# Two attention layers on one NeuronCore: head values on every other partition, row maxima turned by VectorE, local first pass 6 instead of 3 units ahead

## The chip, the core and the metric

The kernel runs on one core of one Trainium2 chip. The metric is device microseconds of one execution. Before the change the median of 3 runs is 2535.94 us (2533.43 to 2537.54). Engine names are those of the profile: PE is TensorE (PEld its weight loads), DVE is VectorE, ACT is ScalarE, POOL is GpSimd, SP is the engine that issues most DMAs; SPq and ACTq are the DMA queues of SP and ACT.

## The reference

Two layers run one after the other on `x` of shape (2, 2048, 256), that is batch B = 2, T = 2048 tokens, D = 256 features. Each layer normalises, computes an attention branch `s` and a gating branch `g`, and adds their product:

```python
xn = _layernorm(x, axis=-1)
s = _L0_attn_ref(xn, ...)            # 16 heads of 16, softmax over all 2048 keys
g = _silu(_L0_ffn_ref(xn, ...))
x = x + s * g
xn = _layernorm(x, axis=-1)
s = _L1_attn_ref(xn, ...)            # 16 heads of 16, keys at most 64 tokens away
g = _silu(_L1_ffn_ref(xn, ...))
x = x + s * g
```

Both attentions are softmax(q k^T * scale) v over heads of 16 values, followed by an output projection. Layer 0 attends to everything ("global" below), layer 1 only to a band ("local"). The two gating branches are not touched by the change. All values are float32.

## The kernel before

**Heads in strips of 32 partitions.** Four heads (a group g of NG = 4) stand together in one q tile and one k tile, each head on HP = 32 partitions: 16 rows of values (HD = 16), then padding rows. In k the padding rows are 1; in q they are 0, except row 16 of each strip (`HD:P:HP`), in which the kernel writes minus the row maximum of the scores. A product k^T q over the 32 rows then gives the score minus the maximum at once. The padded rows come from DRAM: `qd` has 32 rows per head, whose last 16 are filled early in the kernel (L309) with ones for k and zeros for q, and `fetch` (L581) loads all 128 partitions.

**Two passes over the scores.** An item is (batch b, group g, block n of 512 queries): 32 items in each layer. In the first pass PE computes the scores `sq` and DVE takes their maxima into `mx`; in the second PE computes them again as `sk` with the maximum subtracted, ACT takes exponentials into `e` (in the local layer into `xn` and `elast`), and in the local layer POOL cuts the band with four `affine_select` (L688) per unit. PE multiplies with the values (`acc`, L747), to which a column of ones is added so that a row of the result is the softmax denominator.

**Units and leads.** An item has U units: 16 in the global layer (128 keys each in the second pass), 2 in the local layer (256 queries each). The main loop (L945) runs `s` over units; it emits the second pass of unit `s` together with the first pass of unit `s + U + LEAD`. Work that hangs on a unit is put in the dictionary `after` by `at(s, f, ...)` (L856) and emitted behind that unit. Each engine executes what it is given in order. Instructions wrapped in `pin` stay behind everything emitted before them on their engine; the others are ordered by the framework's scheduler.

**How the maximum gets into q.** Global: `turn_max` (L700) negates the 16 columns of `mx` on DVE (L704) and writes them by a DMA in 4-byte pieces to DRAM (`md`, L705); `fetch_max` (L707) brings them back as rows of 512 (L709) three units later. Local: `place_max` (L714), 3 units before the second pass: PE transposes `mx` (L720), ACT negates it into `row` (L723), and ACT's own queue issues the DMA to q (L726).

**After the second pass** the steps of an item follow at fixed hops: `away` writes all 128 rows of `av` to DRAM (`ad`); `compact` loads the 4 denominators' rows as [128 x 16] and the values into `xn`; `invert` takes the reciprocals on DVE (L786); `write` and `spread` send them through DRAM and broadcast them to 64 partitions (`recb`); `divide` multiplies (L802, on POOL, in the local layer on DVE for every other item). `project` (L830) does the output projection once per block when the last group is done. The last items take `last_there` and `last_back` instead.

**Loads of q and k.** There are two q and two k tiles, for group bg and bg + 1. Global: `fetch(bg + 2)` when bg is done. Local: its first half when bg is half done (L880), its second half when bg is done (L882).

**The order of DVE at the start of an attention.** The pools `kq` (q, k) and `vp` (v) are laid on memory of the stage before; POOL fills v with 1 (L515), then DVE copies the values of batch 0 from PSUM (L535) while PE computes them in a ring of 6 banks (L541).

## Time and profile before

| | us |
|---|---|
| median of 3 runs | 2535.94 |
| the profiled execution, its own time | 2538.34 |
| its span (first to last instruction) | 2536.6 |
| layer norms and gating branch of layer 0 | about 0 to 471 |
| global attention | about 471 to 2115 |
| gating branch of layer 1 | about 2115 to 2225 |
| local attention | about 2225 to 2537 |

The profiled execution took 1.7 us more than its span and 2.4 us more than the median of the runs. A row of the profile gives the source line, the engine, the operation, the names and shapes of output and input (partitions x elements), how many there were, and the busy time in all with the mean of one in ns. Small rows that the change touches:

| what | line | count | mean ns |
|---|---|---|---|
| PE transpose of `mx`, local | L720 | 32 | 277 |
| ACT negation into `row`, local | L723 | 32 | 261 |
| ACT issue of `q<-row` | L726 | 32 | 530 to 1128 (median 545) |
| DVE reduction with mask `seen`, local | L674 | 512 | 410 |
| DVE `divide`, local | L802 | 14 | median 900 |
| DVE copy of values | L535 | 33 | 424 |
| POOL fill of v | L515 | 4 | 4045 |

PE is busy 99% of the span. A busy PE is not PE at its peak: the ends of matmuls are modelled. TensorE's granted clock was 0.999 over the span.

### The profile page before, as it was taken

How to read it: one execution, taken by the hardware profiler on the slowest of the kernel's cores; microseconds unless marked ns; L12 is line 12 of the kernel's file. 1: busy time of each engine (PE TensorE's matmuls, PEld its weight loads, DVE VectorE, ACT ScalarE, POOL GpSimd, SP SyncE). 2: the span in 40 equal slices, each digit the busy share in tenths (PEclk: the TensorE clock that was granted, in tenths of full speed). 3: DMA queues.
4: the chain of work that ended last, by engine and by line, in shares of the span. 5: the costliest groups of instructions: out<-in, count | busy, mean ns of one | idle time of the engine just before them, and what ended most of it. 6: DMA issues, size and time to landing. Idle time of an engine off the chain costs nothing.

```text
span 2536.6 us, 47898 instructions
## 1 busy us (share of the span) xinstructions
PE 2513.1 (99%) x18896; PEld 1060.6 (42%) x18896; DVE 1686.2 (66%) x2747; ACT 1620.8 (64%) x3187; POOL 876.6 (35%) x827
## 2 busy tenths in 40 slices
PE   8999999999999999999999999999999999999999
PEld 6444444444333333333333333333333334457766
DVE  4143333157888888888777788788888765238986
ACT  5400000126888888888888888888888886227755
POOL 0000000102444444444444444444444420016887
PEclk9999999999999999999999999999999999999999
DMA  6131111230001001001001001001000002133552
GB/s 243 50 84 51 52 51 39 82 118 14 14 14 43 16 12 44 16 12 44 16 12 43 10 18 44 12 17 43 15 14 10 14 14 63 49 133 108 163 167 81
DMA packets 146353, 129.83 MB, mean 51 GB/s; under 512 B 93456, under 2 KB 97936, under 8 KB 143568
## 3 DMA queue, kind: packets, MB, share of 16 engines
q1 hardware_dynamic: 144256, 125.46, 16.5%
q8 instruction: 148, 2.42, 0.4%
q10 hardware_dynamic: 1872, 1.31, 0.2%
q14 instruction: 77, 0.63, 0.1%
HBM read 80.50 MB, written 45.97 MB: 50 GB/s over the span
## 4 chain that ended last, share of the span: by engine, by line
PE 79%; DMA 1%; ACT 0%; POOL 0%; DVE 0%; issue 0%; ACTq 0%; SPq 0%; POOLq 0%; DVEq 0%
PE sk L667 25%; PE acc L747 22%; PE sq L667 19%; PE pp L477 5%; PE pr L835 2%; PE pp L532 2%; PE po L1027 1%; PE pt L1023 1%; PE po L1035 1%; PE xb L113 0%; PE xb L138 0%; DMA k<-qd 0%; PE of L827 0%; DMA q<-qd 0%; POOL xn L688 0%
## 5 line engine op out<-in xcount | busy, mean ns | idle before, releaser
L679 DVE TENSOR_REDUCE part<-sq 128x2 f32<-128x1024 f32 x1024 | 1207.3, 1221 | 294.3 <-PE sq L667 284.7
L683 ACT ACTIVATE e<-sk 128x512 f32<-128x512 f32 x2048 | 1058.3, 603 | 217.2 <-PE sq L667 197.7
L667 PE MATMUL sk<-q,k 32*128 32x512 f32 (+2 forms) x5632 | 1135.8, 533 | 1.2 <-ACT xn L683 1.0
L667 PE MATMUL sq<-k,q 32*128 32x512 f32 (+2 forms) x5120 | 1129.1, 569 | 0.5 <-DVE part L679 0.5
L761 POOL TENSOR_TENSOR av<-av,more 128x512 f32<-128x512 f32 x459 | 581.4, 1267 | 936.3 <-ACT more L760 931.1
L667 PEld LDWEIGHTS sk<-q,k 32*128 32x128 f32 x5632 | 522.0, 184 | 604.1 <-ACT e L683 512.5
L747 PE MATMUL acc<-e,v 128*32 128x512 f32 x4096 | 546.7, 605 | 0.0
L667 PEld LDWEIGHTS sq<-k,q 32*128 32x128 f32 x5120 | 402.3, 183 | 22.3 <-DVE part L679 13.2
L760 ACT COPY more<-acc 128x512 f32<-128x512 f32 x459 | 268.7, 585 | 1.2 <-PE acc L747 1.0
L747 PEld LDWEIGHTS acc<-e,v 128*32 128x32 f32 x4096 | 81.8, 108 | 388.2 <-ACT e L683 367.8
L461 ACT ACTIVATE gt<-po 128x512 f32<-128x512 f32 x16 | 8.8, 594 | 321.1 <-PE po L457 321.1
L674 DVE CUSTOM_DVE_ANT_0 seen<-sq,mask 128x256 f32<-128x256 f32 (+1 forms) x512 | 176.2, 410 | 53.6 <-PE sq L667 49.2
L467 POOL TENSOR_TENSOR x<-x,up 128x512 f32<-128x512 f32 x16 | 23.1, 1461 | 450.1 <-DVE up L464 277.5
L448 DVE TENSOR_TENSOR xs<-we,px 128x512 f32<-128x512 f32 x64 | 43.9, 686 | 136.2 <-PE px L440 130.3
L688 POOL TENSOR_SCALAR_AFFINE_SELECT xn<-xn 128x512 f32<-128x512 f32 x172 | 106.2, 652 | 77.4 <-ACT xn L683 75.7
L440 PE MATMUL px<-xn,FV 128*128 128x512 f32 x256 | 121.2, 595 | 0.0
L444 PE MATMUL py<-cum,FW 128*128 128x512 f32 x256 | 120.5, 593 | 0.6 <-DVE cum L412 0.6
L424 PE MATMUL po<-pr,UO 128*128 128x512 f32 x256 | 119.0, 592 | 0.0
L683 ACT ACTIVATE xn<-sk 128x512 f32<-128x512 f32 x172 | 89.8, 602 | 41.1 <-PE sk L667 17.9
L450 DVE TENSOR_TENSOR pr<-xs,py 128x512 f32<-128x512 f32 x64 | 44.0, 687 | 64.8 <-PE py L444 64.6
L424 PEld LDWEIGHTS po<-pr,UO 128*128 128x128 f32 x256 | 48.6, 190 | 61.2 <-issue 61.0
L444 PEld LDWEIGHTS py<-cum,FW 128*128 128x128 f32 x256 | 48.4, 190 | 61.5 <-issue 59.8
(195 smaller groups left out, 1604.0 us busy)
## 6 DMA issues: line engine op xcount, KB each, us to landing
we<-wd SPq DMA_DIRECT2D x128, 128.0 KB
ad<-av SPq DMA_DIRECT2D x59, 256.0 KB
qd<-sb SPq DMA_DIRECT2D x48, 256.0 KB
k<-qd SPq DMA_DIRECT2D x10, 1024.0 KB
q<-qd SPq DMA_DIRECT2D x10, 1024.0 KB
xn<-ad SPq DMA_DIRECT2D x59, 128.0 KB
recb<-rd SPq DMA_DIRECT2D x59, 128.0 KB
q<-qd SPq DMA_DIRECT2D x12, 512.0 KB
```

The source lines that it names most:

```text
L424: nc.tensor.matmul(po[oc], UO[:, ch, bass.ts(oc, P)], pr, start=(ch == 0), stop=False)
L440: nc.tensor.matmul(px, FV[:, c, bass.ts(ch, P)], xn[b][:, c, cols], start=(c == 0), stop=(c == NC - 1))
L444: nc.tensor.matmul(py, FW[:, c, bass.ts(ch, P)], cum[:, c, :], start=(c == 0), stop=(c == NC - 1))
L477: nc.tensor.matmul(ps, w[:, c, bass.ts(hf, P)], xn[b][:, c, bass.ts(n, TB)], start=(c == 0), stop=(c == NC - 1))
L667: nc.tensor.matmul(o, lhs, rhs, start=True, stop=True)
L674: nc.vector.tensor_tensor_reduce(seen[:, lo:hi], sq[:, d, t * 2 * P + lo : t * 2 * P + hi], mask[:, lo:hi], 1.0, LOWEST, ALU.add, ALU.max, ...
L679: nc.vector.tensor_reduce(pt[:, pair[0] : pair[1] + 1, t, kb], sq, AX.X, ALU.max)
L683: nc.scalar.activation(e, t, AF.Exp, scale=scale)
L688: nc.gpsimd.affine_select(out=e[:, :, c, :], in_=e[:, :, c, :], compare_op=ALU.is_ge, fill=0.0, base=0, pattern=[[0, 4], [sign, P]], chann ...
L747: nc.tensor.matmul(acc[hp[j], o : o + hi - lo], vs[b][:, kt, vcols(g, j)], es[j][:, lo:hi], start=(r == 0), stop=(r == len(parts) - 1), sk ...
L760: nc.scalar.copy(more, acc)
L761: nc.gpsimd.tensor_tensor(avs[i], avs[i], more, ALU.add)
```

## The change

- The 16 values of a head stand on the even partitions of its strip (0, 2, ... 30) instead of the first 16. The odd rows 1 to 29 are padding, row 31 (`HP - 1`) holds minus the maximum. `qd` in DRAM has only the 16 value rows; the early writes of ones and zeros to it are gone. Instead DVE fills both k tiles with 1 and both q tiles with 0 at the start of each attention, and `fetch` writes every other partition (64 instead of 128 rows).
- Since `fetch` no longer clears the row of the maximum, the first pass multiplies over 31 rows (`hq`), without row 31.
- The values in v stand on every other column; the denominator comes out on row 15 of a strip (`DEN`).
- In both layers the maxima go by `turn_max` and `fetch_max`; `place_max` is gone. `turn_max` negates into every other column of a [128 x 32] tile, DVE transposes that tile in blocks of 32 by 32, and the DMA to `md` has pieces of 128 bytes.
- `LEAD` of the local layer goes from 3 to 6, the value that the global layer had already.
- `away` sends only the 4 rows of denominators to DRAM; `compact` takes the values from `av` directly. The reciprocals are taken on [32 x 64] instead of [128 x 16]. `spread` broadcasts with the 4 heads outermost. Values stand in the order head, value instead of value, head, so the reordering of the weights on the host goes.

```diff
-        [2, B, H, HP, T], F32, name="qd"
+        [2, B, H, HD, T], F32, name="qd"
...
-        zeros = fw.tile([P, TB], F32, name="zeros")
-        nc.vector.memset(zeros, 0.0)
-        for b in range(B):
-            for i, t in ((0, ones), (1, zeros)):
-                for half in range(NC):
-                    nc.sync.dma_start(
-                        out=qd[i, b, bass.ts(half, H // NC), HD:, :], in_=t[:, None, :].to_broadcast([P, NB, TB])
-                    )
...
-        LEAD = 3 if local else 6
+        LEAD = 6
+        DE = 64
...
-            ad = [dr.tile([NG, HP, TB], F32, name=f"ad{i}", tag=f"ad{i}") for i in range(3)]
+            ad = [dr.tile([NG, TB], F32, name=f"ad{i}", tag=f"ad{i}") for i in range(3)]
...
-            md = [dr.tile([NG * TT, P], F32, name=f"md{i}", tag=f"md{i}") for i in range(2)]
+            md = [dr.tile([NG * TT, NG, HP], F32, name=f"md{i}", tag=f"md{i}") for i in range(2)]
+
+            for k, q in zip(ks, qs):
+                nc.vector.memset(k, 1.0)
+                nc.vector.memset(q, 0.0)
...
+                s = vs[b][p0:p1, c, :]
                 copy(
-                    vs[b][p0:p1, c, : H * HV].rearrange("p (h w) -> p h w", w=HV)[:, :, :HD],
+                    bass.AP(s.tensor, s.offset, [s.ap[0], [HV, H], [2, HD]]),
...
+            hq = [slice(j * HP, (j + 1) * HP - 1) for j in range(NG)]
...
-                    nc.sync.dma_start(out=t[:, to], in_=qd[i, b, bass.ts(g, NG), :, s].rearrange("h w t -> (h w) t"))
+                    nc.sync.dma_start(out=t[::2, to], in_=qd[i, b, bass.ts(g, NG), :, s].rearrange("h w t -> (h w) t"))
...
-                                        q1[hp[j], bass.ts(qt, P)], k1[hp[j], qt * P + lo : qt * P + hi],
+                                        q1[hq[j], bass.ts(qt, P)], k1[hq[j], qt * P + lo : qt * P + hi],
...
+            nmx = [mp.tile([P, NG * TT, 2], F32, name=f"nmx{i}", tag=f"nmx{i}", bufs=1) for i in range(2)]
+            for m in nmx:
+                nc.vector.memset(m, 0.0)
+
             def turn_max(i):
 
                 mx, _ = part.pop(i)
-                nmx = mp.tile([P, NG * TT], F32, name="nmx", tag="nmx")
-                pin(nc.vector.tensor_scalar(nmx, mx.rearrange("p j t -> p (j t)"), -1.0, None, ALU.mult))
-                pin(nc.sync.dma_start(out=md[i % 2].rearrange("j p -> p j"), in_=nmx))
+                m = nmx[i % 2]
+                pin(nc.vector.tensor_scalar(m[:, :, 0], mx.rearrange("p j t -> p (j t)"), -1.0, None, ALU.mult))
+                turned = mp.tile([P, HP], F32, name="tmx", tag="tmx")
+                pin(nc.vector.transpose(turned, m.rearrange("p i e -> p (i e)")))
+                pin(nc.sync.dma_start(out=md[i % 2].rearrange("i s r -> s i r"), in_=turned[::2]))
 
             def fetch_max(i):
 
                 pin(nc.sync.dma_start(
-                    out=tiles(i)[0][HD:P:HP, bass.ts(items[i][2], TB)],
-                    in_=md[i % 2].rearrange("(j t) p -> j (t p)", t=TT),
-                ))
-
-            def place_max(i):
...
+                    out=tiles(i)[0][HP - 1 : P : HP, bass.ts(items[i][2], TB)],
+                    in_=md[i % 2].rearrange("(j t) s r -> j (t s r)", t=TT),
                 ))
...
-                pin(nc.sync.dma_start(out=ad[i % 3].rearrange("j w f -> (j w) f"), in_=avs.pop(i)))
+                pin(nc.sync.dma_start(out=ad[i % 3], in_=avs[i][DEN::HP]))
...
-                divs[i] = op.tile([P, NG * TB // P], F32, name="dn", tag="dn", bufs=3)
-                pin(nc.sync.dma_start(out=divs[i], in_=flat(ad[i % 3][:, HD, :])))
-                pin(nc.sync.dma_start(out=together(*items[i]), in_=ad[i % 3][:, :HD, :].rearrange("j d f -> d j f")))
+                divs[i] = op.tile([NG * TB // DE, DE], F32, name="dn", tag="dn", bufs=3 if local else 1)
+                pin(nc.sync.dma_start(out=divs[i], in_=flat(ad[i % 3])))
+                pin(nc.sync.dma_start(out=together(*items[i]), in_=avs.pop(i)[::2]))
...
-                pin(nc.sync.dma_start(out=divs[i], in_=rd[i % 3][None, :, :].to_broadcast([HD, NG, TB])))
+                pin(nc.sync.dma_start(out=divs[i], in_=rd[i % 3][:, None, :].to_broadcast([NG, HD, TB])))
...
-                if local:
-                    at(i * U - LEAD, place_max, i)
-                else:
-                    at(i * U - LEAD, turn_max, i)
-                    at(i * U - LEAD + 3, fetch_max, i)
+                at(i * U - LEAD, turn_max, i)
+                at(i * U - LEAD + 3, fetch_max, i)
```

More of the change, by code (lines that the diff above doesn't have):

```diff
@@ L25 @@
 HV = HD + 1
+DEN = HD - 1
 TB = 512
@@ L481, in keys_queries @@
         nc.scalar.activation(sb, ps, AF.Identity, bias=bias[:, hf : hf + 1])
-        nc.sync.dma_start(out=qd[i, b, bass.ts(hf, H // NC), :HD, bass.ts(n, TB)], in_=sb)
+        nc.sync.dma_start(out=qd[i, b, bass.ts(hf, H // NC), :, bass.ts(n, TB)], in_=sb)
     def attention(A, scale, local, final, start=None, projected=False):
@@ L663, in scores @@
                                 pieces.append((
-                                    when, sq[:, d], q1[hp[j], bass.ds(n1 * TB + t * P, P)], k1[hp[j], bass.ts(kb, TB)]
+                                    when, sq[:, d], q1[hq[j], bass.ds(n1 * TB + t * P, P)], k1[hq[j], bass.ts(kb, TB)]
                                 ))
@@ L698, in attention @@
             pin = tc.keep_in_program_order
+            nmx = [mp.tile([P, NG * TT, 2], F32, name=f"nmx{i}", tag=f"nmx{i}", bufs=1) for i in range(2)]
+            for m in nmx:
+                nc.vector.memset(m, 0.0)
             def turn_max(i):
                 mx, _ = part.pop(i)
-                nmx = mp.tile([P, NG * TT], F32, name="nmx", tag="nmx")
-                pin(nc.vector.tensor_scalar(nmx, mx.rearrange("p j t -> p (j t)"), -1.0, None, ALU.mult))
-                pin(nc.sync.dma_start(out=md[i % 2].rearrange("j p -> p j"), in_=nmx))
+                m = nmx[i % 2]
[3 more added lines that the diff above has]
+                pin(nc.sync.dma_start(out=md[i % 2].rearrange("i s r -> s i r"), in_=turned[::2]))
             def fetch_max(i):
                 pin(nc.sync.dma_start(
-                    out=tiles(i)[0][HD:P:HP, bass.ts(items[i][2], TB)],
-                    in_=md[i % 2].rearrange("(j t) p -> j (t p)", t=TT),
-                ))
-            def place_max(i):
-                b, g, n = items[i]
-                q = tiles(i)[0]
-                mx, _ = part.pop(i)
-                ps = pm.tile([NG * TT, P], F32, name="pmx", tag="m")
-                nc.tensor.transpose(ps, mx.rearrange("p j t -> p (j t)"), ident)
-                row = mp.tile([NG * TT, P], F32, name="row", tag="row", bufs=2 if local else 1)
-                if local:
-                    pin(nc.scalar.activation(row, ps, AF.Copy, scale=-1.0))
-                else:
-                    nc.vector.tensor_scalar(row, ps, -1.0, None, ALU.mult)
-                pin((nc.scalar if local else nc.sync).dma_start(
-                    out=q[HD:P:HP, bass.ts(n, TB)].rearrange("j (t c) -> j t c", c=P), in_=row
+                    out=tiles(i)[0][HP - 1 : P : HP, bass.ts(items[i][2], TB)],
+                    in_=md[i % 2].rearrange("(j t) s r -> j (t s r)", t=TT),
                 ))
@@ L771, in away @@
             def away(i):
-                pin(nc.sync.dma_start(out=ad[i % 3].rearrange("j w f -> (j w) f"), in_=avs.pop(i)))
+                pin(nc.sync.dma_start(out=ad[i % 3], in_=avs[i][DEN::HP]))
             def flat(d):
-                return d.rearrange("j (r e) -> r j e", r=P // NG)
+                return d.rearrange("j (r e) -> (j r) e", e=DE)
             def compact(i):
-                divs[i] = op.tile([P, NG * TB // P], F32, name="dn", tag="dn", bufs=3)
-                pin(nc.sync.dma_start(out=divs[i], in_=flat(ad[i % 3][:, HD, :])))
-                pin(nc.sync.dma_start(out=together(*items[i]), in_=ad[i % 3][:, :HD, :].rearrange("j d f -> d j f")))
+                divs[i] = op.tile([NG * TB // DE, DE], F32, name="dn", tag="dn", bufs=3 if local else 1)
+                pin(nc.sync.dma_start(out=divs[i], in_=flat(ad[i % 3])))
+                pin(nc.sync.dma_start(out=together(*items[i]), in_=avs.pop(i)[::2]))
             def invert(i):
@@ L810, in last_there @@
                     nc.tensor.transpose(ps[:, t].rearrange("p j w -> p (j w)"), av[:, bass.ts(t, P)], ident)
-                rec = op.tile([P, TT, NG], F32, name="dn", tag="dn", bufs=3)
-                o = divs[i] = op.tile([P, TT, HD, NG], F32, name="over", tag="recb", bufs=2)
-                nc.vector.reciprocal(rec, ps[:, :, :, HD])
+                rec = op.tile([P, TT, NG], F32, name="rec", tag="rec", bufs=2)
+                o = divs[i] = op.tile([P, TT, NG, HD], F32, name="over", tag="recb", bufs=2)
+                nc.vector.reciprocal(rec, ps[:, :, :, DEN])
                 nc.vector.tensor_tensor(
-                    o.rearrange("p t d j -> p t j d"), ps[:, :, :, :HD],
-                    rec[:, :, :, None].to_broadcast([P, TT, NG, HD]), ALU.mult,
+                    o, ps[:, :, :, ::2], rec[:, :, :, None].to_broadcast([P, TT, NG, HD]), ALU.mult
                 )
@@ L822, in last_back @@
                 lo = g % 2 * NG * HD
-                o = divs.pop(i).rearrange("p t d j -> p t (d j)")
+                o = divs.pop(i).rearrange("p t j d -> p t (j d)")
                 ps = pm.tile([P, TB], F32, name="of", tag="m")[lo : lo + NG * HD, :]
@@ L859, in attention @@
             for i, (b, g, n) in enumerate(items):
-                if local:
-                    at(i * U - LEAD, place_max, i)
-                else:
-                    at(i * U - LEAD, turn_max, i)
-                    at(i * U - LEAD + 3, fetch_max, i)
+                at(i * U - LEAD, turn_max, i)
+                at(i * U - LEAD + 3, fetch_max, i)
                 end = (i + 1) * U
@@ L1122, in _attn_arrays @@
 def _attn_arrays(l, wq, wk, wv, bq, bk, bv, wo_t, bo):
-    apart = lambda m: m.reshape(NG, NG, HD, -1).transpose(0, 2, 1, 3).reshape(m.shape)
     cols = lambda v: np.asarray(v).reshape(NC, P).T
@@ L1129, in _attn_arrays @@
         f"wv{l}": wv,
-        f"wo{l}": apart(np.asarray(wo_t).T),
+        f"wo{l}": np.asarray(wo_t).T,
         f"bq{l}": cols(bq),
         f"bk{l}": cols(bk),
-        f"bv{l}": cols(apart(np.asarray(bv))),
+        f"bv{l}": cols(bv),
         f"bo{l}": cols(bo),
```

## The prediction

> **What bounds the kernel now.** I read the page first: engines' shares and the chain that ended last.

> ```profile
> span 2536.6 us, 47898 instructions
> PE 2513.1 (99%) x18896; PEld 1060.6 (42%) x18896; DVE 1686.2 (66%) x2747; ACT 1620.8 (64%) x3187; POOL 876.6 (35%) x827
> ...
> PE 79%; DMA 1%; ACT 0%; POOL 0%; DVE 0%; issue 0%; ACTq 0%; SPq 0%; POOLq 0%; DVEq 0%
> ```

> PE sets the end; DMA, which the change cuts most, has 1% of the chain. Bytes saved are worth nothing by themselves. But 66% for DVE is a mean over stages, so I took busy times by stretches, one in the middle of the global attention, one in the local (columns: stretch, length, then busy us and count of PE, PEld, DVE, ACT, POOL, then clock and DMA):

> ```profile
> 1000.00:1500.00 500.00, 500.00 (x4013) 169.80 (x4008) 400.95 (x371) 421.92 (x829) 221.40 (x175) 1.00 0.08 21
> ...
> 2331.00:2409.00 78.00, 77.43 (x1540) 61.60 (x1544) 71.93 (x399) 57.61 (x132) 66.88 (x102) 1.00 0.52 160
> ```

> Global: DVE 80%, POOL 44%: room. Local: PE 99%, **DVE 92% and POOL 86%**. The starts of `acc` in the timeline give the local item: 2318.17, 2324.57, 2330.96, 2337.47, so 6.47 us (two units) on average, of which DVE works 71.93 / 78 x 6.47 = 5.97. Its slack is 0.5 us per item. That is the number on which the local stage hangs.

> **Global stage: nothing, 0 (-2 to +2).** The first pass with 31 rows must still run four heads side by side. The timeline has products over 16 rows (two accumulators on two strips) beside ones over 128:

> ```profile
> 249.79 1.88 PE L440 MATMUL px<-xn,FV 128*128 128x512 f32 x4
> ...
> 256.75 1.13 PE L457 MATMUL po<-wT,bO 16*128 16x512 f32 x4
> ```

> Four instructions of 16 rows take 1.13 us against 1.88, so a partly filled strip overlaps with its neighbour; 31 rows should too. DVE gains one transpose per item and a longer reciprocal (below), 0.5 us per 46.8 us. In this stage DVE idles 0.57 us in each unit of 2.92 before the next `sq`; the reciprocal of now lowers that idle to 0.41 in its unit, the longer one leaves about 0.1. It fits. Shorter DMAs change nothing: the wait of SP for `md<-nmx` (10 us each, by the waits of SP) is three units ahead and PE has no idle there. The early writes of ones and zeros (8 MB, 33 to 67 us) lie under a PE that is busy 19.90 and 20.00 of 20 us there.

> **Start of the local attention: +3 (0 to +4).** Four fills of 2048 or 2176 columns now stand on DVE ahead of the copies of v. Rows:

> ```profile
> L302 DVE MEMSET ones<- 128x512 f32 x1 | 0.5, 485 | 0.1
> ...
> L557 DVE MEMSET mask<- 128x256 f32 x1 | 0.3, 272 | 0.0
> ```

> (485 - 272) / 256 = 0.83 ns per column and 59 ns fixed: 1.76 for q, 1.87 for k, 7.3 us in all. [...] The memory comes free at 2224.7 (POOL's fill of v waits for `po` until then), DVE finishes its last two updates at 2226.05, so the copies of v start at 2233.3 instead of 2228.95. PE has 6 banks at 0.86 us each, filled at 2230.5; it then waits some 3 us. With one or two fills in DVE's idle time before 2224.4 less is left; at best 0. In the global attention the same fills cost nothing: DVE idles 29.41 us before its first copy of v.

> **The maxima of the local layer.** Gone, per item: on PE a transpose, from its start to the next `sk` 0.20 us (2487.56 to 2487.76); on ACT 0.26 for `row` and 0.55 for the issue of the DMA. ACT has room (57.61 of 78), so this pays only where ACT is blocked. It is, because ACT's queue must wait for the load of q:

> ```profile
> 2463.97 4.83 DMA q<-qd
> 2468.87 0.54 ACTq L726
> ```

> (The chain over this stretch.) Exponentials stand behind that issue, and PE's longest wait, 1.2 us, is there: -1.3 in all. On SP, three units ahead, the fetch blocks nobody's exponentials. Behind the new DMA of `turn_max` on SP stand `write`, `spread` and loads; SP issues some 5 DMAs of 0.55 us per item now, 6 to 7 after, in 6.47 us.

> Added on DVE, per item, each a guess only as far as its row:
> - Reciprocal on 64 columns instead of 16. Rows: 174 ns for 4 columns, 253 for 16, 354 for 32; 6.3 ns per column gives 556 for 64, so **+0.31**.
> - Transpose of [128 x 32]: no row. Below: a fill of 64 columns, 112 ns. [...] Nearest row: a DVE copy of 32 columns, 190. I take 0.2.
> - Negation, 165 ns. But:

> ```profile
> L704 DVE TENSOR_SCALAR nmx<-mx x32: 165/166/1252, 580.2 to 2052.2; 128x16 f32<-128x16 f32 x32
> ...
> 2052.11 1.28 POOL L761 TENSOR_TENSOR av<-av,more 128x512 f32<-128x512 f32 x1 [1.66 <-ACT more L760]
> 2052.17 1.25 DVE L704 TENSOR_SCALAR nmx<-mx 128x16 f32<-128x16 f32 x1
> ```

> All but one took 166 ns; the one that met a POOL instruction took as long as that. [...] This speaks against moving it from ACT to DVE here. I take 0.42; up to 1.5 if it must wait for a whole run of four selects (2.4 us).

> Sum 0.93, less some 0.1 because small DVE instructions overlap (0.17 to the next start where 0.25 is shown): 0.83. DVE then needs 5.97 + 0.83 = **6.80 us per item where the item takes 6.47**. DVE becomes the bound: +0.33. This holds in the items where both passes run and no projection fills PE: 32, less 4 in the run-up, 4 of batch 0's last group and the first: 23 x 0.33 = **+7.6** (bounds: 0.55 added, +1; 1.6 added, +25). In the rest (9 items) PE keeps its 0.20: -1.8.

> **Lead 6 instead of 3: +1.4 (-1 to +3).** Three more first passes before the first exponential, 3 x 1.1 us beside projections that fill PE: +3.3. Three fewer units with both passes: -3 x 3.23. Three more at the end with the second pass alone, where ACT (4 x 0.53 + 0.4) and POOL (2.4 + 0.3) need 2.6: +7.8. What gets tighter: the second half of a k tile, loaded when the group two before ends, is needed at unit 3 instead of 6. Issue 2318.2, need about 2326; k took 5.3 us for 512 KB in the chain, now half the bytes. It fits by 3 to 4 us.

> **Values out of `av`, 4 rows of denominators:** DMAs off the path. [...]

> **Sum** against the execution's own 2538.3: +3.0 + 1.4 + 7.6 - 1.8 - 1.3 = +8.9, 2547.2. That execution lies 2.4 above the median of the runs, so I predict **2544.8**.

> **Rivals.**
> 1. DVE's additions fit into its slack (0.55 or less), and PE's lost transpose counts everywhere: 24 x -0.1 to -0.2, -1.8, -1.3, lead and fills 0 to +2. For it: DVE idles 0.2 to 0.7 us per unit in items without `divide`; against: items with it have none left. 2528 to 2535, say **2532**.
> 2. Slower by one mechanism: the negation waits for POOL's whole run. A `divide` on DVE did so at 2503.59, 5.07 us; against: the median of 14 is 0.90. From 1.0 us of added wait per item it decides: 23 more, **2568**.
> 3. Loads of q and k late with the greater lead, because SP stands before a `turn_max` that waits for a late DVE: some 2 us in each of 6 groups on top, **2557**. Against: the margin above.
> 4. The 31-row product is not packed: hundreds of us. The 16-row row excludes it; under 1%.

> **How the numbers follow.** Forecast 0.47, rival 1 0.30, rival 2 0.13, rival 3 0.10. No change is within 0.2% (5 us, about what a measurement tells). Rival 1 is faster in two thirds of its cases and no change in the rest; the forecast's low end gives another 0.1 of no change. Faster 0.20, same 0.20, slower 0.60. The range of 8 in 10, 2530 to 2563, leaves out the best of rival 1 and the worst of rival 2; the forecast's own is 2539 to 2555.

> **What would show it.** DVE near 98% busy in the middle of the local stage, items of 6.7 to 6.9 us, PE waiting for DVE's `seen` there; reciprocals of 0.55; negations well over 0.17 in the local part; a gap of about 3 us on PE at 2230; global items still 46.8 us. It is wrong if local items fall to 6.3 (the DVE sum is too high), if the global item lengthens (a view I took as room is not), or if PE waits for loads of q and k.

## The result and the profile after

The changed kernel takes 2547.11 us (median, 2542.03 to 2550.26) where the kernel before takes 2536.92 (2533.43 to 2539.51; six executions of each): ratio 1.004, 95% interval 1.0029 to 1.0051. It is slower by 10.2 us, outside the 0.2% that can be told from no change. The forecast was 2544.8. On another chip, where the kernel before is slower, the two differ by 0.1% only (experiment 5).

The page of the changed kernel, the lines that answer to those shown of before:

```profile
span 2541.3 us, 47980 instructions
...
PE 2511.5 (99%) x18864; PEld 1054.5 (41%) x18864; DVE 1739.1 (68%) x2854; ACT 1616.8 (64%) x3155; POOL 876.3 (34%) x827
...
PE 77%; DVE 2%; issue 1%; POOL 0%; DMA 0%; ACT 0%; SPq 0%; POOLq 0%; DVEq 0%; ACTq 0%
```

PE still sets the end, but DVE, which had 0% of the chain that ended last, now has 2%. DMA moves 90 MB instead of 130. The same stretch of the local layer as before:

```profile
2331.00:2409.00 78.00, 77.55 (x1452) 58.30 (x1450) 77.50 (x400) 54.53 (x115) 61.97 (x98) 1.00 0.29 87
```

DVE (the third busy time of the row) went from 71.93 to 77.50 of 78 us. Yet that is only one of the places in which the time changed. I cut both profiles at events that both have (starts of PE's products) and compared the pieces:

| piece | before | after | difference | predicted |
|---|---|---|---|---|
| start to the global layer's first weighted product `acc` | 599.7 | 594.0 | -5.6 | 0 |
| from there to the local layer's first product (values) | 1625.7 | 1622.6 | -3.1 | 0 |
| from there to the local layer's first `acc` | 73.5 | 83.6 | +10.2 | +6.3 |
| from there to the end | 237.8 | 241.0 | +3.2 | +2.6 |

The first row is no effect of the change. In the profile of before PE ran at half clock in two windows of 3.41 us, near 21 and 472 us (granted clock 0.83 from 20 to 30 us and from 465 to 475 us); the profiled execution of the changed kernel had neither (1.00 in both). Run 6 below starts as the changed kernel does and has both windows: its first `acc` comes at 599.6, as that of before (599.7). So the spans differ by 4.7 us and the medians by 10.2: -3.1 + 10.2 + 3.2 is 10.3. (Of the predictions, +6.3 is the fills' 3.0 and the lead's 3.3, and +2.6 is 7.6 - 1.8 - 1.3 and the rest of the lead's term, 1.4 - 3.3.)

**The local layer's start.** Timeline of the changed kernel (start, duration, instruction, in brackets the idle time before it and what ended it):

```profile
2216.64 5.59 PE L529 MATMUL pp<-wv,xn 128*64 128x256 f32 x24 [0.69 <-ACT gt L1024]
...
2216.92 1.87 DVE L509 MEMSET k<- 128x2176 f32 x1 [0.40 <-DVE x L1026]
...
2224.13 1.76 DVE L510 MEMSET q<- 128x2048 f32 x1 [0.38 <-issue]
...
2225.92 2.21 DVE L533 COPY v<-pp 64x256 f32<-64x256 f32 x6
...
2226.41 12.26 PE L529 MATMUL pp<-wv,xn 128*128 128x256 f32 x44 [4.17 <-DVE v L533]
```

Before, the first 49 of these products ran without a gap:

```profile
2225.32 10.99 PE L532 MATMUL pp<-wv,xn 128*64 128x256 f32 x49 [0.69 <-ACT gt L1039]
```

In the changed kernel the fills hold DVE from 2216.92 to 2225.89; the copies of v follow, and PE, whose six banks are full, waits 4.17 us. Windows over the same place (PE busy is the first busy time, PE's granted clock the third number from the end):

```profile
2215.00:2225.00 10.00, 6.55 (x27) 4.31 (x25) 7.68 (x6) 1.19 (x2) 8.89 (x8) 0.97 0.35 105
2225.00:2230.00 5.00, 3.59 (x9) 2.88 (x10) 3.50 (x8) 0.00 (x0) 0.99 (x3) 0.50 0.70 210
2230.00:2235.00 5.00, 5.00 (x22) 4.32 (x21) 2.13 (x5) 0.00 (x0) 0.00 (x0) 0.88 0.01 3
```

At half clock for a part of each window, 0.97, 0.50 and 0.88 come to 0.6, 5 and 1.2 us: two windows of 3.41 us, from about 2224.4, inside PE's gap, to 2231.2.

**The middle.** Groups of DVE between 2330 and 2413 us (count, busy us, mean ns, idle before):

```profile
L708 DVE TENSOR_SCALAR nmx<-mx 128x16 f32<-128x16 f32 x12 | 7.4, 616 | 0.0
L775 DVE RECIPROCAL dn<-dn 32x64 f32<-32x64 f32 x13 | 7.0, 536 | 0.1
...
L710 DVE STREAM_TRANSPOSE tmx<-nmx 128x32 f32<-128x32 f32 x12 | 2.5, 212 | 0.4
```

The reciprocal and the transpose cost what was predicted (0.56 and 0.2); the negation costs 0.62 where 0.42 was taken. Six of the twelve negations took 157 or 158 ns and six 556 to 1499, and each of these six ends 0.03 or 0.04 us after the end of one of POOL's `affine_select`. The longest waits for a whole run of four, which ends at 2348.32, it at 2348.36:

```profile
2345.93 2.39 POOL L687 TENSOR_SCALAR_AFFINE_SELECT xn<-xn 128x512 f32<-128x512 f32 x4
...
2346.86 1.50 DVE L708 TENSOR_SCALAR nmx<-mx 128x16 f32<-128x16 f32 x1
```

The idle time of DVE before its reductions, 6.6 us in this stretch, is gone (the kernel before, then the changed one):

```profile
L674 DVE CUSTOM_DVE_ANT_0 seen<-sq,mask 128x256 f32<-128x256 f32 x176 | 63.4, 417 | 6.6 <-PE sq L667 5.1 <-PE sk L667 1.5
...
L673 DVE CUSTOM_DVE_ANT_0 seen<-sq,mask 128x256 f32<-128x256 f32 x169 | 60.4, 409 | 0.0
```

The twelve items between the tenth and the 34th unit take 82.8 us, 6.90 each, before 78.6, 6.55 each.

**A new wait.** The waits of PE between 2200 and 2541 us (us in total, times, longest):

```profile
PE pp L529 <- DVE v L533: 4.2, 1, 4.2
PE sk L666 <- DMA q<-md: 3.0, 2, 2.0
...
PE sk L666 <- ACT xn L682: 0.5, 1, 0.5
```

The waits for ACT of before (1.2, 1.0) are down to 0.5; in their place the scores wait 3.0 us for the maxima. The timeline says why:

```profile
2453.88 0.40 SPq L835 DMA_DIRECT2D out<-x  x1
2454.37 0.58 SPq L785 DMA_DIRECT2D recb<-rd  x1
2455.00 0.60 SPq L771 DMA_DIRECT2D dn<-ad  x1
2455.66 0.50 SPq L772 DMA_DIRECT2D xn<-av  x1
2456.20 0.53 SPq L715 DMA_DIRECT2D q<-md  x1
...
2459.89 0.79 PE L666 MATMUL sk<-q,k 32*128 32x256 f32 x2 [2.03 <-DMA q<-md]
```

The timeline is that of the longer wait, 2.0 us; the other, 1.0 us at 2503, has no output ahead of it. SP issued these five one behind the other, from 2453.88 to 2456.20. The DMA of the output stood there waiting for POOL's last addition to x (SP waits 25.6 us in all for that, seven times), and the fetch came last of what stood behind it.

### The profile page after: what moved, and what is told of

It is laid out like the page before. It is cut to its first block, busy times and chain, and to the rows that moved or that the text cites. A ratio compares the mean times of both kernels' runs of the same rounds, so it can differ in the third digit from the quotient of the medians.

```text
span 2541.3 us, 47980 instructions
## 1 busy us (share of the span) xinstructions
PE 2511.5 (99%) x18864; PEld 1054.5 (41%) x18864; DVE 1739.1 (68%) x2854; ACT 1616.8 (64%) x3155; POOL 876.3 (34%) x827
## 3 DMA queue, kind: packets, MB, share of 16 engines
q1 hardware_dynamic: 56292, 85.83, 10.5%
## 4 chain that ended last, share of the span: by engine, by line
PE 77%; DVE 2%; issue 1%; POOL 0%; DMA 0%; ACT 0%; SPq 0%; POOLq 0%; DVEq 0%; ACTq 0%
PE sk L666 24%; PE acc L737 22%; PE sq L666 19%; PE pp L469 4%; PE pr L823 2%; PE pp L529 2%; DVE seen L673 1%; PE po L1012 1%; PE pt L1008 1%; PE po L1020 1%; PE xb L114 0%; PE xb L139 0%; DMA q<-md 0%; POOL elast L687 0%; PE of L815 0%
## 5 line engine op out<-in xcount | busy, mean ns | idle before, releaser
L666 PE MATMUL sq<-k,q 31*128 31x512 f32 (+2 forms) x5120 | 1130.4, 570 | 0.6 <-DVE part L678 0.5
L666 PEld LDWEIGHTS sq<-k,q 31*128 31x128 f32 x5120 | 398.3, 184 | 29.1 <-DVE part L678 12.6
L440 DVE TENSOR_TENSOR xs<-we,px 128x512 f32<-128x512 f32 x64 | 43.9, 686 | 136.3 <-PE px L432 131.3
```

The lines of the kernel that those rows point to most:

```text
L666: nc.tensor.matmul(o, lhs, rhs, start=True, stop=True)
```

## Experiments

The changed kernel is the base unless said otherwise. Besides the time, three pieces of each profile are used: the **global** layer from its first to its last `acc`, the **run-up** (local layer's first product to its first `acc`), and the **middle** (the twelve items named above). Before: 1510.9, 73.5, 78.6; changed: 1508.0, 83.6, 82.8. The runs fell on several chips. On that of runs 1 to 4 the kernel before took 2545.6 us, on that of runs 5 to 9 2544.7 and 2544.3, on that of runs 10 and 11 2558.1; which chip the 2536.9 of the result comes from is not known; it is called the first below. That the kernel before differs so much turned out to be a result of its own.

**1. Fills of the local layer on POOL.**

```diff
-            for k, q in zip(ks, qs):
-                nc.vector.memset(k, 1.0)
-                nc.vector.memset(q, 0.0)
             for t in vs:
                 nc.gpsimd.memset(t, 1.0)
+            for k, q in zip(ks, qs):
+                (nc.gpsimd if local else nc.vector).memset(k, 1.0)
+                (nc.gpsimd if local else nc.vector).memset(q, 0.0)
```

> The changed kernel with the four fills of q and k of the local layer on POOL, behind its fills of v, instead of on DVE. Theory A (the fills hold back the copies of v; PE's gap of 4.17 us there lets the clock fall to one half for two windows of 3.41 us): the gap goes and the half clock with it, 4.2 + 2.4 = 6.6 us less, median about 2540.5 us, and the first exponential's unit starts some 74 + 3.3 us after the local layer's first product instead of 84.3. Rival B (the half clock has nothing to do with the gap): only 4.2 less, 2543, half-clock windows still near the start of the local layer. Rival C (loads of q and k, now behind POOL's fills, become late in their place): less than 2 us gained, PE waits at its first scores at 2246.

2537.6 us, ratio to before 0.9966 (0.9954 to 0.9978). Its timeline:

```profile
2219.00 8.27 POOL L509 MEMSET v<- 128x4879 f32 x2 [91.74 <-PE po L1020]
2219.58 15.23 PE L529 MATMUL pp<-wv,xn 128*64 128x256 f32 x68 [0.69 <-ACT gt L1024]
2223.20 2.43 DVE L533 COPY v<-pp 64x256 f32<-64x256 f32 x6 [2.90 <-POOL v L509]
```

68 products without a gap, no half clock there, run-up 76.9 instead of 83.6: 6.8 us, theory A. Of these 4.2 are the gap; the other 2.6 went with the half clock, of which 4.8 us lay behind the gap, a loss of 2.4 at half speed. Rival C falls too: the loads of q and k, now behind POOL, are in time.

**2. No negation.** k's padding becomes -1, so the maxima themselves go into q, and the reductions write straight into the tile that is transposed.

```diff
-                nc.vector.memset(k, 1.0)
+                nc.vector.memset(k, -1.0)
...
-                            mp.tile([P, NG, TT], F32, name="mx", tag="mx"),
+                            nmx[i1 % 2].rearrange("p (j t) e -> p j t e", t=TT)[:, :, :, 0],
...
-                pin(nc.vector.tensor_scalar(m[:, :, 0], mx.rearrange("p j t -> p (j t)"), -1.0, None, ALU.mult))
```

> The changed kernel without the negation: k's fill is -1 instead of 1, the maxima are written straight into the tile that is transposed, so DVE loses one instruction per item in both layers. Theory A (DVE is the bound in about 12 local items of 6.87 us): 0.17 us less per item by the usual row, up to 0.42 with its waits for POOL, 12 times: 2 to 5 us less, about 2543.5; items 6.5 to 6.7. Rival B (the middle of the local layer is longer because of the greater lead or late transfers, not of DVE): no difference, within 1 us of 2547.1. The global layer stays as it is by both.

2544.0 us, 0.9994 (0.9986 to 1.0003); the changed kernel did not run on this chip, and against its 2545.4 on the next one the medians alone would not settle it. The items do: the middle takes 79.1 instead of 82.8, 0.31 per item, and every other item falls to 6.16. DVE is what they waited for.

**3. Denominators as 128x16.**

```diff
-        DE = 64
+        DE = 16
```

> The changed kernel with the denominators as 128x16 again instead of 32x64; only the shape of the reciprocal and of the DMAs around it differ. Theory A: reciprocal 0.25 instead of 0.53, 0.28 us less for DVE per item, in some 12 DVE-bound items: 3.4 us less, about 2543.7; those items take 6.6 instead of 6.87. Rival B (DVE is not what lengthens them): no difference, within 1 us of 2547.1. The global layer's items stay 46.8 us by both.

2544.1 us, 0.9996 (0.9988 to 1.0004). The reciprocal takes 245 ns again, 0.29 less, but the middle falls by 0.11 per item only (81.5): in the same stretch the negation now takes 754 ns instead of 616. What DVE no longer spends on one instruction it partly spends waiting in the other.

**4. The kernel before with the lead of 6 alone.**

```diff
-        LEAD = 3 if local else 6
+        LEAD = 6
```

> The kernel before with one edit: the first pass of the local layer runs 6 units ahead instead of 3. The prediction's term: +1.4 us (-1 to +3), so about 2538.3: three first passes more ahead of the first exponential (+3.3), three units less with both passes, three more at the end with the second pass alone. Items in the middle stay near 6.5 us since DVE's work is that of before. Rival: the greater lead is itself what makes the middle longer (loads of q and k late): +4 or more, PE waiting for loads of q or k.

2551.2 us, 1.002 (1.0012 to 1.0028): 5.6 us, more than the prediction's range. The run-up is 4.2 longer, and ACT stands still twice (1.7 and 3.3 us of PE's time). ACT's timeline at the second:

```profile
2465.89 0.26 ACT L723 ACTIVATE row<-pmx 16x128 f32<-16x128 f32 x1
2469.73 0.55 ACTq L726 DMA_DIRECT2D q<-row  x1
2470.38 2.06 ACT L683 ACTIVATE xn<-sk 128x512 f32<-128x512 f32 x4 [4.22 <-DMA recb<-rd]
```

The row of maxima is ready at 2466.15, and its DMA goes at 2469.73; four exponentials stand behind it. It waits on a completion semaphore that it is to use itself and that the broadcast `recb<-rd`, issued on SP at 2465.15, still held until 2469.65. (The load of q, my suspect, had landed at 2466.59. In the profile of before, what held ACT's DMA until 2468.8 was such a load, issued at 2463.97, by way of a semaphore that both use: the trace has number 102 as what ACT waits for and as what both transfers end on.) The loads of q and k go out just before, so a late SP transfer stops the exponentials as long as ACT's queue carries the maxima. The change moves them to SP.

**5. The changed kernel again, twice on one other chip.**

> The changed kernel itself again, as the yardstick of this set: the kernel before took 2536.9 us on one chip and 2545.6 on another, and the long units that its profile shows in the global layer (7 of 32 items on the first chip, about 20 of 32 on the second) are in none of the three variants of the changed kernel. If they are the difference between the chips, the changed kernel takes about 2547 on both, and its ratio to the kernel before depends on the chip: 1.004 on the first, about 1.000 where before takes 2545. If a chip is slower for every kernel alike, the ratio is 1.004 again.

> The changed kernel again, on the same chip as the run above. Theory A: about 2545 to 2547 on this chip too, so that the ratio of the two is 1.004 to 1.005 whatever before takes here: the loss that the change makes in the local layer without its gain in the global one.

2545.4 us in both, ratios 1.0007 (0.9998 to 1.0016) and 1.0012 (1.0003 to 1.0021): before took 2544.7 and 2544.3 there. The changed kernel takes within 2 us of its 2547.1 of the first chip; the kernel before takes 7 to 8 us more than there. What it loses is then likely something that the change takes away, and the second row of the table (-3.1 us, where 0 was predicted) says that it is in the global layer. There the profile of before shows this, at item 20 (timeline; `acc` starts a unit every 2.92 us):

```profile
1532.96 0.38 SPq L705 DMA_DIRECT2D md<-nmx  x1
...
1542.86 1.07 PE L747 MATMUL acc<-e,v 128*32 128x512 f32 x8
...
1543.01 0.53 SPq L709 DMA_DIRECT2D q<-md  x1
...
1546.79 1.07 PE L747 MATMUL acc<-e,v 128*32 128x512 f32 x8
```

A unit of 3.93 us. No unit of the changed kernel is long there. In this profile 6 such units in the first 30 items cost 3.7 us, in that of run 4 14 cost 9.4, and each lies where the transfer of the maxima in 4-byte pieces ends. PE is never shown idle there: in the unit above it is busy 3.93 of 3.93 us, so the profile has laid the loss into instructions. Nor are the maxima late in the profile of before: the fetch `q<-md`, which takes some 2 us, goes 3.0 us or more ahead of the first scores of its item, in the long units too.

**6. 4-byte pieces again, in the global layer only.**

```diff
                 m = nmx[i % 2]
                 pin(nc.vector.tensor_scalar(m[:, :, 0], mx.rearrange("p j t -> p (j t)"), -1.0, None, ALU.mult))
+                if not local:
+                    pin(nc.sync.dma_start(out=md[i % 2].rearrange("i s r -> (s r) i"), in_=m[:, :, 0]))
+                    return
```

> The changed kernel with, in the global layer alone, the maxima written out as before: straight from the tile of 128x16, in pieces of 4 bytes, without the transpose. Theory A (the 10 to 12 us of these 2048 pieces are what lengthens a unit in the global layer, always the one in which the transfer ends): the long units come back at that place, +3 to +9 us on the changed kernel, as much as before loses on that chip. Rival B (the prediction's own step: shorter transfers are worth nothing in the global layer, and what the kernel before loses there has another cause, such as the filled rows or the loads of q and k): no long units, no difference within 1 us.

2557.7 us, 1.0039 (1.0025 to 1.0053), 12.3 above the changed kernel on the same chip (8.4 between the two profiled executions). The global layer goes from 1508.0 to 1516.3 us. The long units are back at their place:

```profile
1968.97 1.06 PE L740 MATMUL acc<-e,v 128*32 128x512 f32 x8
1971.90 1.07 PE L740 MATMUL acc<-e,v 128*32 128x512 f32 x8
1975.68 1.07 PE L740 MATMUL acc<-e,v 128*32 128x512 f32 x8
```

Here md<-nmx was issued at 1961.98 and q<-md at 1973.40. With transfers of 11 to 12 us a few fetches of this run go only some 2 us ahead of the first scores, so that a part of its smaller losses may be scores that wait. SP's waits for the transfer, first of before, then of the changed kernel (us in total, times, longest):

```profile
SPq L709 <- DMA md<-nmx: 262.5, 26, 10.4
```

```profile
SPq L715 <- DMA md<-tmx: 38.5, 32, 1.4
```

**7. The kernel before with this part alone**: transpose and 128-byte pieces in the global layer, all else as before.

```diff
...
-                nmx = mp.tile([P, NG * TT], F32, name="nmx", tag="nmx")
-                pin(nc.vector.tensor_scalar(nmx, mx.rearrange("p j t -> p (j t)"), -1.0, None, ALU.mult))
-                pin(nc.sync.dma_start(out=md[i % 2].rearrange("j p -> p j"), in_=nmx))
+                m = nmx[i % 2]
+                pin(nc.vector.tensor_scalar(m[:, :, 0], mx.rearrange("p j t -> p (j t)"), -1.0, None, ALU.mult))
+                turned = mp.tile([P, HP], F32, name="tmx", tag="tmx")
+                pin(nc.vector.transpose(turned, m.rearrange("p i e -> p (i e)")))
+                pin(nc.sync.dma_start(out=md[i % 2].rearrange("i s r -> s i r"), in_=turned[::2]))
...
```

> The kernel before with this one part of the change alone: in the global layer the maxima are turned by a transpose on DVE and written out in pieces of 128 bytes; the local layer and everything else are those of before. Theory A (the pieces of 4 bytes are the only reason why the kernel before takes 2537 on one chip, 2545 on two and 2558 on a fourth): the transfer takes 1.8 us instead of 10 to 12, PE's first scores of an item no longer wait for q<-md, the global layer takes 1472.7 us from its first to its last weighted product on whatever chip, and the median is 2533 to 2536, so the ratio to before is 0.999 where before takes 2537, 0.996 at 2545, 0.991 at 2558. Rival B (the difference between the chips lies elsewhere in the kernel before, such as its 16 KB of filled rows or its longer loads): the ratio is 0.998 to 0.999 on each chip.

2536.2 us where before takes 2544.3: 0.9968 (0.9956 to 0.9979), theory A for this chip; on the others it was not run. No unit of the global layer is long (1507.2 us in all; the 1472.7 of the expectation end fourteen units earlier), and on the same chip the whole change takes 2545.4. So the change is two things of opposite sign: a part worth 3 us on the first chip and 8 on this one, and a loss of about 9 to 13 in the local layer.

This run has the local layer of before, but its middle takes 80.6 us, not 78.6. The row of maxima is ready at 2372.09 and ACT's DMA goes at 2373.79, held by a load of q as in run 4, here with the lead of 3:

```profile
2375.17 1.08 PE L754 MATMUL acc<-xn,v 128*32 128x128 f32 x24 [1.52 <-ACT elast L683]
```

So the 78.6 is no fixed property of the kernel before: against this profile the middle of the changed kernel is 2.2 us longer, against the first 4.2.

**8. Fills on POOL, no negation and 128x16 together** (the edits of 1 to 3).

> Three edits together: the local layer's fills of q and k on POOL, no negation (k's fill is -1), denominators as 128x16. Theory A (DVE bounds the middle of the local layer, and the fills its start): local items fall to 6.2 to 6.4 us in the middle (12 items x 0.5 = 6 us less), the start loses its gap (6.6 us less): about 12 us under the changed kernel on this chip, ratio to before 0.993 to 0.996. Rival B (one bound only gives way to another: POOL's selects or ACT take over at once): middle items stay above 6.6, 8 us at most.

2532.0 us, 0.9948 (0.9935 to 0.996), 13.4 below the changed kernel in the same set. Run-up 77.1, middle 77.4, 6.45 per item: close to theory A (6.2 to 6.4), under what rival B allows (6.6). One of the new waits stays:

```profile
PE sk L666 <- DMA q<-md: 2.2, 1, 2.2
```

**9. The fetch first, the output on POOL's queue.** From here on run 8 is the base; the maxima also get a third buffer in DRAM.

```diff
...
+            for i in range(len(items)):
+                at(i * U - LEAD + 3, fetch_max, i)
             for i, (b, g, n) in enumerate(items):
...
-                    nc.sync.dma_start(
+                    nc.gpsimd.dma_start(
                         out=out[:, bass.ds(b * T + n * TB, TB)].rearrange("(c p) n -> p c n", p=P),
...
```

> The three edits of the run before, and the fetch of the maxima first among the DMAs of its step, three buffers for them in DRAM instead of two, and the output's DMA of all but the last item on POOL's queue, so that SP does not wait for POOL's x ahead of the fetch. Theory A (the 2.0 us for which PE's scores wait for q<-md at the end of batch 0's projections come from SP standing before that output DMA): this wait goes, 2 to 3.5 us less than the run before (the gap, and at times a half-clock window after it). Rival B (the fetch is late because the transpose is late, or because the transfer itself is slow there): the wait stays, no difference[...].

2531.7 us, 0.9941 (0.9929 to 0.9954): no difference from run 8. The wait for q<-md is gone, so its cause was what stood ahead of it on SP; but POOL pays 0.72 us for an issue, after 0.30 us of idle time, and comes late, and a product waits 0.5 for its `divide`, scores 0.6 for DVE. The local layer takes 310.5 us, in run 8 310.1.

**10. Run 9 with the output on SP again, two steps later; and 11. the same with a lead of 4.**

```diff
...
+                    if final and i < len(items) - 1:
+                        at(end + DEL + hops[-1] + NC - 1 + 2, send, i)
...
```

```diff
...
-        LEAD = 6
+        LEAD = 4 if local else 6
...
-                at(i * U - LEAD + 3, fetch_max, i)
+                at(i * U - LEAD + (1 if LEAD == 4 else 3), fetch_max, i)
...
```

> The three edits (fills on POOL, no negation, 128x16), the fetch of the maxima first in its step and three buffers in DRAM for them, and the output's DMA of all but the last item again on SP, but two steps behind the last update of x that it waits for. Theory A (with the output on POOL's queue, the wait for q<-md of 2.2 us was traded for POOL's issues of 0.72 us, after which a product waited 0.5 us for POOL's divide and scores 0.6 us for DVE): neither wait is there, about 1 to 2 us less than with the output on POOL's queue, ratio to before about 0.994 on a chip where before takes 2545 and 0.997 where it takes 2537. Rival B (SP's queue is late there for other transfers too): the wait for q<-md comes back, at the item in which batch 0's projections end.

> The same with a lead of 4 units instead of 6 in the local layer, the fetch one step behind the transpose. By the prediction's own term (three units more cost +1.4, of which the run-up +3.3): two units less give 0.9 us, the run-up is 2.2 shorter and the end takes back the rest. Rival B (the lead of 6 is needed: the new way through DRAM, transpose, 1.8 us, fetch, 2.0 us, and the queue between them no longer fits into 4 units of 3.1 us once DVE runs late): PE's scores wait for q<-md in most items, +5 us or more.

2533.1 us, 0.9901 (0.9884 to 0.9918), and 2529.5 us, 0.9897 (0.9878 to 0.9915), on a chip where before takes 2558. The wait for q<-md is in neither. The local layer takes 309.2 us in both, 1.3 less than in run 9, as run 10's theory A had it. With the lead of 4 the run-up is 3.4 us shorter (73.7 against 77.1; 2.2 were expected), and items of 7.1 to 7.6 us give that back. The medians of the two differ by less than their spread. The changed kernel did not run on this chip; on two others it took 2545 to 2547.

## Why the prediction came out right, step by step

The forecast lay 2.3 us under the median, and the side was right. That it lay so near is in part luck: of its terms some held, and three were off in ways that cancelled (global stage -3.1 where 0 was taken, fills 6.8 for 3.0, DVE-bound items 4.2 for 7.6). The side, too, is that of the first chip: on the second the ratio was 1.0007 and 1.0012, within 0.2%, because there the term taken as 0 is worth some 8 us.

- **Global stage, 0 (-2 to +2): wrong.** The step that failed reads "Shorter DMAs change nothing: the wait of SP for `md<-nmx` ... is three units ahead and PE has no idle there." Three units is how far ahead the fetch is emitted, not how far ahead it runs: DVE's negation is done some 14 us before the item's first scores, and 10 to 12 us of transfer and 2 of fetch use nearly all of it. In the profile of before that was still in time, and its units were long all the same: a transfer for which PE does not wait was taken for one that costs PE nothing. And "no idle" was read from a view that cannot show it. Runs 6 and 7 give +8.3 us in the layer and -8 us in the median for that transfer alone; on the first chip it is the -3.1 of the table. DVE's extra transpose does fit, as predicted: without 4-byte pieces every unit outside the projections and the last item is 2.93 us.
- **Fills +3.0 (0 to +4): the mechanism right, the size too small.** The durations (1.87, 1.76), the full banks and the gap came as worked out, the gap 4.17 instead of about 3: between the fills DVE stands idle for 0.38 to 0.40 us each time, which a sum of durations leaves out, and one of its last updates lies among them, so that the four hold it for 9.0 us, not 7.3. The term that was missing is the clock: the other 2.6 us of run 1, which removes gap and half clock together.
- **DVE-bound items, 23 x 0.33 = 7.6: right per item, wrong in number.** 12 items x 0.35 = 4.2 against the first profile, 2.2 against that of run 7. (The starts that the prediction quotes give 6.43 us an item, not 6.47, and the twelve items 6.55; with 6.55 its sum is 6.04 + 0.83 = 6.87, where 6.90 was measured.) In the others PE kept its 0.2 (mostly 6.0 to 6.4 where before took 6.4 to 6.5). All 23 were taken to cost DVE what the stretch read costs it, but the negation waits for POOL so much mainly there: it takes 616 ns in the middle, 354 between 2300 and 2331 us, 161 between 2469 and 2495. Run 2 shows that it is DVE.
- **Negation 0.42: a guess, and still low.** By its usual row it costs 0.17, and the 0.25 that makes it 0.42 is a price that no run shows. The runs showed 0.62 on average: six of twelve negations end with a `select` of POOL, at 556 to 1499 ns, while the other six took 157 or 158. Run 2 took 0.31 per item away; the row alone would have given 0.17.
- **Lead +1.4 (-1 to +3): right in the new kernel, wrong as a property of the old.** The run-up's +3.3 was measured as 3.4 (run 1 less before), but as a net figure: a unit of lead costs more than the 1.1 taken, 1.4 in the kernel before (4.2 for three, run 4) and 1.7 in run 10 (3.4 for two). In all, run 11 against run 10 puts two units at 0.0. In the kernel before the same edit costs 5.6 us (run 4), since there ACT's queue waits for transfers of SP: near to rival 3, in a place that the change empties.
- **ACT's stall -1.3: gone, and replaced.** "On SP, three units ahead, the fetch blocks nobody's exponentials" is true. The prediction named what stands behind the new DMA on SP and not what stands ahead of the fetch: an output DMA that waits for POOL. That cost 2.0 us of waiting and, behind it, another half-clock window (granted clock 0.67 from 2460 to 2465 us).
- **Rivals.** Rival 1 needed additions within 0.55 us per item; DVE got about 1.1. Rival 2 (the negation waits 1.5 us) is true of single ones (the longest took 1.50), not on average. Rival 3's loads of q and k were in time in the changed kernel. 31 rows run four abreast like 32: the units have not grown (median 2.925 us from `acc` to `acc` in the global layer before, 2.927 after).

What was predicted to show it: DVE at 98% (99%), items of 6.7 to 6.9 (6.90 in twelve), reciprocals 0.55 (0.54), negations well over 0.17 (0.62), a gap of 3 us (4.17) were all there; "PE waiting for `seen`" was not shown as a wait, only as longer units, and the global item was not the 46.8 of before at all places, but of before without its long units.

## What to carry to other kernels

A unit's length between two starts of the same product tells what a view of waits cannot: losses of 0.2 to 2.0 us in a unit never showed as PE's idle time. For a transfer that is "units ahead", compare when its data are made with when they are due, do not take one that is in time for one that costs nothing, and read what stands ahead of it in its queue, not only what stands behind. On an engine that has 0.5 us of slack per item, a small instruction is priced by what it waits for there (0.62), not by its usual row (0.17); and when a change mixes a gain with a loss, the part that gains is worth running by itself.

## What the runs showed of the hardware that was not expected

**4-byte pieces hold PE up; by what path is open.** The trace's DMA records have a queue of 16 KB packets marked as instructions. I take them for PE's: 148 packets in the kernel before, where PE and PEld together have 37,792 instructions, some 255 a packet. In the global layer one comes every 15.6 us, which is 5.3 units. Between 620 and 1236 us and between 1425 and 2004 us, where no projections are, the intervals are at most 16.7 us in all eleven profiles of kernels with 128-byte pieces. With 4-byte pieces, 11 of 77 in the kernel before and 16 of 77 in run 6 are over 17 us, up to 20.4. Five of the six long units of before come right behind such a late packet:

```
packet, us           since the last   unit, us          (2.92 otherwise)
1541.08-1542.36      17.85            1542.86-1546.79   3.93
1588.84-1589.76      17.81            1590.67-1594.83   4.16
1683.44-1684.85      17.51            1685.51-1688.92   3.41
1824.24-1825.26      18.35            1826.40-1829.57   3.17
1870.80-1872.26      17.96            1873.44-1876.65   3.21
```

At the first, PE's semaphore updates, in the units before at most 1.03 us apart, stop at 1541.05 and go on at 1543.30, while the 2048 pieces, whose records end by 1535.2, land at 1542.40. That PE ran out of instructions would fit these five. It does not fit all: the sixth long unit (637.68, 3.34 us) has its packet at 638.65, only 15.5 us after the last and after PE's updates had gone on (638.31), and six of the eleven late packets have no long unit behind them. Runs 6 and 7 (+8.3 us in the layer, -8 us in the median) show that the pieces cost this time; the late packets may be its cause or another effect of the same transfer.

**The kernel before differs by 21 us between chips** (2537 to 2558), the kernels without 4-byte pieces hardly: the changed kernel took 2547.1, 2545.4 and 2545.4 on two of them, and runs 9 and 10, which differ in the output's DMA alone, 2531.7 and 2533.1 on two chips between which before differs by 14. In before the transfer took 10.5 us on the first chip, in run 4 on the next 11.3. That the pieces are the whole difference between chips is likely from this, but run 7, which would show it, ran on one chip only.
